# Layer 0 of a four-layer network: a unit's sums are folded half a group sooner, their copies and some small transfers change queues

## The chip, the cores and the metric

One core of a Trainium2 chip runs the whole network in one launch. The metric is the device time of that core in microseconds (us), the median of three runs. Five engines work side by side, each taking its own instructions in order: TensorE (PE, matrix products), VectorE (DVE), ScalarE (ACT), GpSimd (POOL) and SyncE (SP). ACT, POOL and SP also issue the DMAs; which one issues a DMA decides in whose order it stands.

## The reference

Four layers run one after the other on images of 512 channels. Only layer 0 is touched by the change. It is attention with a sampled set of 64 keys for each of 2 x 8 heads and a learned position bias, and the bias is what costs time:

```python
pos = grid_q[:, :, None, :] - grid_kv[:, None, :, :]          # 1024 queries x 64 keys x 2
bias = jnp.sign(pos) * jnp.log1p(jnp.abs(pos))
bias = jax.nn.relu(bias @ cpb_w1 + cpb_b1)                    # 2 -> 128
bias = jax.nn.relu(bias @ cpb_w2 + cpb_b2)                    # 128 -> 128
bias = (bias @ cpb_w3 + cpb_b3)                               # 128 -> 1
sim = jnp.einsum('bhid,bhjd->bhij', qh, kh) + bias
attn = jax.nn.softmax(sim, axis=-1)
out = jnp.einsum('bhij,bhjd->bhid', attn, vh)
```

So a small network with 128 hidden values runs on 16 heads x 1024 queries x 64 keys. The keys' places come from a convolution of the queries (`off`), and `grid_sample` fetches the keys' inputs there.

## The kernel before

**Units, groups, half groups.** Layer 0 is a hand-ordered program (`layer0`): PE, DVE, ACT and POOL take their instructions in the order in which the Python code writes them. A unit `u` (0 to 15) is one head of one image. It has eight groups `o` (0 to 7) of eight keys, and each group has two halves of four keys. The loop at L190 runs over these half groups; there are 16 in a unit, and I number them `it` 0 to 15, so `it = 2 * o + half`. Units 2p and 2p+1 share a "pair" (one tile of 128 channels), whose queries, key places, keys and values are made ahead by generators in the list `front`; the softmax and output of a finished unit are generators in the list `after`. At the end of each half group one step of `after` is run, and one of `front` as well if that step of `after` allows it.

**One half group.** `first_hidden` (L739 to L762) makes the first hidden layer on DVE for the next half group. `second_hidden` (L764 to L818) then multiplies with `w2s` on PE (L780) in four quarters `q`, each into a PSUM tile `hp` of which there are three; ACT reads each with a Relu (L794) and so frees the PSUM tile. Quarter 0 is followed by a second ACT pass (L797 or L799). The quarters are added up: 1 += 0 by an accumulating DMA that POOL issues (L804), 3 += 2 by POOL (L808), and 3 += 1 by POOL one half group later (`join`, L811). In some halves DVE takes a quarter instead of ACT: `late`, quarter 3 (L789; second halves of groups 1 and 2, in odd units of groups 1 to 4), and `early`, quarter 2 (L792; second halves of groups 0 and 7).

**Folds and sums.** Both halves' quarter 3 are the two parts of one tile with the tag `two`, of which there are three, so group `g` writes into the tile of group `g-3`. A group's tile is folded over its partitions 128 to 64 to 32 to 16 by three accumulating DMAs that POOL issues (L814, L836, L839), and then SP copies the 16 rows that are left into a sum tile (L846, two DMAs). These later steps are generators in `refolds`: `refold_more` runs a step at quarter 1 of each later half group, and the copies at the end of the half group named in the entry, here the second half of group `g+2`. Each unit has two sum tiles, `sum{u}_0` for even and `sum{u}_1` for odd groups, with the tag `sum` and three buffers. The tiles go round these three buffers in the order 0_0, 0_1, 1_0, 1_1 and so on, so `sum{u}_1` lies where `sum{u-1}_0` was.

**A finished unit's sums.** While unit `u` runs, the two sum tiles of unit `v = u - 1` become the bias of its attention (for `u` from 1 to 14): ACT multiplies by a sign (L222), POOL issues two accumulating folds (`keys_rows`, L851 and L853, 128 to 64 to 32 partitions), and ACT issues two DMAs that copy the 32 rows into `rows` (L857). Before the change this is written at the end of `it` 3 for `sum_0` and `it` 5 for `sum_1`, the folds come at `it` 5 and 6, and 7 and 8, the copies at the end of `it` 7 and 9, and `attend` starts at the end of `it` 11.

**Small transfers.** For each pair `offsets` writes the logarithms (`logs`) and the sampling places (`spots`) to DRAM, and `sampled` reads `spots` back into all partitions (`at`); DVE uses `at` at L604. `load` brings `lb` back from `logs` (ACT issues three of four, L676). The first three of these go through `send`, which issues on SP:

```python
def send(self, to, what):
    with self.behind(self.gathered):
        self.nc.sync.dma_start(to, what)
```

Of the kernel before, what the change touches and what calls it, by code (L numbers as in the profile page):

```python
# [18 lines left out]
P = 128  # L19
# [4 lines left out]
HF = 512  # L24
# [33 lines left out]
class Net:  # L58
# [40 lines left out]
    def layer0(self):  # L99


        nc, io = self.nc, self.io
        with ExitStack() as ctx:
# [45 lines left out]
            with self.tc.manual_schedule(engines=engines):  # L149
# [40 lines left out]
                for i, (u, o, half) in enumerate(quads):  # L190
                    self.half = half
                    if o == 2 and half == 1 and u % 2 == 0 and u // 2 + 1 < BP:
                        nxt = pairs[u // 2 + 1]
                        front += [self.offsets(nxt, u // 2 + 1, ps), self.sampled(nxt, u // 2 + 1, ps)]
                    h1 = ready
                    if i + 1 < len(quads):
                        if quads[i + 1][1:] == (7, 0) and u + 1 < 2 * BP:
                            self.advance(front, lambda: "logs" in pairs[(u + 1) // 2])
                        ready = self.first_hidden(*quads[i + 1], pairs, tables)
                    last_set = u == last and o >= 4  # L200
                    if half == 0:
                        if o == 0:
                            before, sums = sums, []
                        if o % 4 == 0:
                            group = []
                        if i + 2 < len(quads):
                            both = self.two_tiles(f"h2_{u}_{o}3")
                            group.append([both[:, 0, :], both[:, 1, :], both])
                        else:
                            group.append([self.four_rows(f"h2_{u}_{o}{n}3") for n in range(2)])  # L210
                        if o < 2:
                            sums.append(self.four_rows(f"sum{u}_{o}"))
                    self.second_hidden(i, u, o, half, h1, group[-1], i + 1 == len(quads), last_set)
                    if half == 1 and not last_set:
                        end = i + (3 if u == last else 4)
                        self.refolds.append((i + 2, end, end, self.refold(group[-1][2], sums[o % 2], o // 2, u == last)))
                    v = u - 1
                    if half == 1 and o in (1, 2) and 0 <= v < last - 1:
                        z = before[o - 1]
                        if o == 1:  # L220
                            rows = self.soft.tile([P, HF], F32, tag="pt", name=f"rows{v}")
                        nc.scalar.activation(z, z, AF.Copy, scale=self.last_sign)  # L222
                        self.refolds.append((i + 2, i + 4, i + 4, self.keys_rows(z, rows, o - 1)))
                    if half == 1 and o == 2 and v >= 0:
                        sims[v] = ps_s.tile([P, HF], F32, tag="sim", name=f"sim{v}")
                        if v == last - 1:
                            self.sum_product(sims[v], self.thrice, True, before)
                        self.advance(front, lambda: "v" in pairs[v // 2])
                        self.keys_queries(v, pairs[v // 2], sims[v], v < last - 1)
                    if v >= 0 and (o, half) == ((5, 1) if v < last - 1 else (2, 1)):  # L230
                        if v == 8:
                            self.advance(after, lambda: False)
                            att = [apool.tile([P, N], F32, tag=f"att{t}", name=f"att{v}_{t}") for t in range(CT)]
                        after.append(self.attend(v, pairs[v // 2], sims[v], att, ps, rows if v < last - 1 else None))
                        if v % 8 == 7:
                            after.append(self.projection(ps, att, ow, v // 8))
                    elif half == 1 and u == last and o == 5:
                        sims[u] = ps_s.tile([P, HF], F32, tag="sim", name=f"sim{u}")
                        self.sum_product(sims[u], self.twice[:, 16:48], True, sums)
                    elif half == 1 and u == last and o == 7:  # L240
                        self.sum_product(sims[u], self.folded[:, 8:40], False, [one[0] for one in group[:2]])
                    self.refold_more(i, True)
                    if not self.step(after):
                        self.step(front)
# [156 lines left out]
    def offsets(self, m, bt, ps):  # L401
# [3 lines left out]
        nc = self.nc  # L405
# [33 lines left out]
        o = self.bank[:, 256:258]  # L439
        for par in range(2):  # L440
            rows = slice(par * DH, (par + 1) * DH)
            nc.tensor.matmul(o[rows, :], lhsT=ge[rows, :], rhs=self.colr("pw", 2)[rows, :], start=True, stop=True)
        tanh, at = self.bank[:, 258:260], self.bank[:, 260:262]
# [15 lines left out]
        log = self.fpool.tile([P, 2, W], F32, tag="log", name=f"log{b}{t}")  # L459
# [14 lines left out]
        else:  # L474
            nc.vector.tensor_tensor(log, log, sign, ALU.mult)
        logs = self.dram.tile([P, 2 * W], F32, tag="logs", name=f"logs{b}{t}")
        self.send(logs, log.rearrange("p d x -> p (d x)"))
        spots = self.dram.tile([P, 2], F32, tag="spots", name=f"spots{b}{t}")

        g = self.fpool.tile([P, 2], F32, tag="g", name=f"g{b}{t}")  # L480
        nc.scalar.activation(g, at, AF.Identity, scale=W / 2.0, bias=self.grid[:, G_MID : G_MID + 1])
        self.send(spots, g)
        m["log"], m["logs"], m["spots"] = log, logs, spots
        yield

# [1 line left out]

        return nullcontext() if ins is None else self.tc.issue_after(ins.ins)

    def send(self, to, what):  # L490

        with self.behind(self.gathered):
            self.nc.sync.dma_start(to, what)

# [92 lines left out]
    def sampled(self, m, bt, ps):  # L587
# [3 lines left out]
        nc = self.nc  # L591
        b, t = divmod(bt, CT)
        spots = self.fone.tile([P, 2 * NJ, 2], F32, tag="spots", name=f"at{b}{t}")
        self.send(spots, m["spots"].rearrange("k d -> (k d)").partition_broadcast(P))
        if "xT" not in m:
            self.sampling(m, bt)
            nc.scalar.copy(m["xT"], self.turn(m, bt, ps))
# [25 lines left out]
        for n in range(NB):  # L623
            for par in range(2):
                rows = slice(par * DH, (par + 1) * DH)
# [17 lines left out]
        for par in range(2):  # L643
            rows = slice(par * DH, (par + 1) * DH)
# [25 lines left out]
    def load(self, u, c, pairs, early):  # L670

        logs = pairs[u // 2]["logs"].rearrange("(a j c i) e -> a c j (i e)", a=2, j=2, c=4)[u % 2, c]
        got = self.lpool.tile([P, 2, 8, 2, W], F32, tag="logs", name=f"lb{u}{c}")
        to, what = got.rearrange("p j i d x -> p j (i d x)"), logs.unsqueeze(0).to_broadcast([P, 2, 16 * W])
        if early:
            self.nc.scalar.dma_start(to, what)  # L676
        else:
            self.send(to, what)
        return got

    def table(self, u, o, pairs, tables):
# [166 lines left out]
    def keys_rows(self, z, to, jj):  # L848

        nc = self.nc  # L850
        nc.gpsimd.dma_start(z[0::2], z[1::2], accum_op=ALU.add)  # L851
        yield
        nc.gpsimd.dma_start(z[0::4], z[2::4], accum_op=ALU.add)  # L853
        yield
        for h in range(2):
            at = h * NJ + jj * 32
            nc.scalar.dma_start(to[at : at + 32, :], z[0::4, h * HF : (h + 1) * HF])  # L857

    def sum_product(self, sim, lhsT, start, zs):

# [1348 lines left out]
```

## Time and profile before

| what | value |
|---|---|
| time, median of 3 runs | 3255.38 us (3253.26 to 3260.8) |
| time of the profiled execution | 3257.2 us |
| its span from first to last instruction | 3255.5 us |
| half groups of layer 0 | from about 27 us to about 1935 us |
| granted TensorE clock, mean | 0.996 |
| PE busy over the span | 98% |
| ACT, DVE, POOL busy over the span | 59%, 76%, 73% |

Layer 0 fills the first 24 of the page's 40 slices. The other layers are untouched by the change, so the difference of the two kernels is to be looked for in the first 1935 us. A busy share is a mean over a stage; what delays an engine is read from its idle time and from what ended it.

### The profile page before, as it was taken

What the parts mean: (1) busy time and instruction counts of PE and PEld (TensorE: products, weight loads), DVE (VectorE), ACT (ScalarE), POOL (GpSimd) and SP (SyncE); (2) the same over time, 40 slices, a digit from 0 to 9 for tenths busy, and PEclk for the clock granted to TensorE, in tenths of its full rate; (3) what the DMA queues carried; (4) which work ended last, traced back from release to release, by engine and by line L of the source; (5) the groups of instructions that cost most, each with busy time, mean ns of one, the idle gap of its engine ahead of it and who ended that gap; (6) DMA issues with size and microseconds to landing.
All of it is one profiled execution on the core that took longest, in us unless ns stands there. A gap on an engine that the chain in (4) does not pass through costs nothing.

```text
span 3255.5 us, 58764 instructions
## 1 busy us (share of the span) xinstructions
PE 3205.5 (98%) x23956; PEld 1216.4 (37%) x23956; DVE 2475.8 (76%) x2834; ACT 1906.6 (59%) x1985; POOL 2361.8 (73%) x1664
## 2 busy tenths in 40 slices
PE   9999999999999999999999999999999999999999
PEld 4323233233333333343332334444455533455333
DVE  7878878878878678888887865575565689855897
ACT  7877777877877577787877761111231466213662
POOL 7989988989989789989988965333243458634575
PEclk9999999999999999999999999999999999999999
DMA  6787787787787677787787863111000100000001
GB/s 168 161 174 156 155 172 156 155 165 162 160 166 158 130 155 158 154 169 164 156 168 157 164 142 116 47 44 39 1 1 1 40 1 1 15 1 14 1 1 53
DMA packets 96590, 341.91 MB, mean 105 GB/s; under 512 B 19888, under 2 KB 22064, under 8 KB 79216
## 3 DMA queue, kind: packets, MB, share of 16 engines
q0 software_dynamic: 56224, 244.88, 39.5%
q1 hardware_dynamic: 23600, 62.68, 5.8%
q10 hardware_dynamic: 16480, 30.42, 3.4%
q8 instruction: 193, 3.16, 0.4%
q14 instruction: 93, 0.76, 0.1%
HBM read 67.37 MB, written 4.46 MB: 22 GB/s over the span
## 4 chain that ended last, share of the span: by engine, by line
PE 62%; POOL 17%; DMA 7%; DVE 7%; issue 4%; ACT 2%; ACTq 0%; SPq 0%; POOLq 0%; DVEq 0%
PE hp L780 25%; POOL h L811 7%; PE s L1742 5%; PE o L1771 5%; POOL h L808 5%; DMA h<-h 3%; POOL h L804 2%; DMA sum<-h 2%; ACT h L794 2%; PE qk30P L1517 1%; PE qk20P L1517 1%; PE m_7P L1026 1%; PE m_5P L1026 1%; PE m_4P L1026 1%; PE m_2P L1026 1%
## 5 line engine op out<-in xcount | busy, mean ns | idle before, releaser
L780 PE MATMUL hp<-h,w2s 128*32 128x512 f32 x16384 | 1803.3, 595 | 35.1 <-ACT h L794 32.8
L794 ACT ACTIVATE h<-hp,magb 128x1024 f32<-128x1024 f32 x950 | 1044.5, 1109 | 428.8 <-PE hp L780 327.3
L753 DVE CUSTOM_DVE_ANT_1 h<-tx,bank 128x1024 f32<-128x1024 f32 (+1 forms) x1028 | 1180.7, 1211 | 120.3 <-PE hp L780 84.4
L780 PEld LDWEIGHTS hp<-h,w2s 128*32 128x32 f32 x16384 | 564.1, 110 | 1240.3 <-issue 1074.6
L811 POOL TENSOR_TENSOR h<-h,h 128x1024 f32<-128x1024 f32 x254 | 739.2, 2910 | 15.9 <-DMA h<-h 13.8
L808 POOL TENSOR_TENSOR h<-h,h 128x1024 f32<-128x1024 f32 x209 | 656.8, 3142 | 6.1 <-ACT h L794 6.1
L804 POOL DMA_DIRECT2D h<-h x227 | 295.3, 1301 | 139.5 <-ACT h L794 138.2
L1746 ACT ACTIVATE e<-s 128x1024 f32<-128x1024 f32 x256 | 262.0, 1025 | 180.9 <-PE s L1742 175.3
L1771 PE MATMUL o<-e,v 64*64 64x512 f32 x2048 | 265.2, 589 | 2.2 <-DVE q L1810 2.2
L1742 PE MATMUL s<-q,k 64*64 64x512 f32 x2048 | 265.9, 591 | 0.0
L799 ACT ACTIVATE h<-h,flip 128x1024 f32<-128x1024 f32 x182 | 209.6, 1152 | 6.0
L1753 POOL TENSOR_TENSOR some<-some,e 128x1024 f32<-128x1024 f32 x64 | 167.6, 2618 | 26.7 <-ACT e L1746 24.2
L836 POOL DMA_DIRECT2D h<-h x124 | 174.3, 1405 | 16.6 <-DMA h<-h 9.6
L1751 POOL TENSOR_TENSOR some<-e,e 128x1024 f32<-128x1024 f32 x32 | 76.1, 2378 | 141.3 <-DVE sum L1760 106.3
L814 POOL DMA_DIRECT2D h<-h x127 | 162.9, 1283 | 6.0 <-issue 3.9
L1758 DVE TENSOR_TENSOR sum<-sum,e 128x1024 f32<-128x1024 f32 x64 | 123.7, 1932 | 29.8 <-ACT e L1746 27.1
L839 POOL DMA_DIRECT2D h<-h x120 | 137.3, 1144 | 5.9 <-DMA h<-h 5.4
L996 POOL TENSOR_TENSOR mlp_w<-mlp_w 128x512 f32<-128x512 f32 x16 | 22.6, 1413 | 159.4 <-DMA mlp_w<-in_mlp_w 127.3
L1771 PEld LDWEIGHTS o<-e,v 64*64 64x64 f32 x2048 | 77.8, 133 | 145.0 <-issue 135.2
L1742 PEld LDWEIGHTS s<-q,k 64*64 64x64 f32 x2048 | 76.5, 133 | 133.2 <-issue 117.6
L789 DVE SCALAR_TENSOR_TENSOR h<-hp,under,h 128x1024 f32<-128x1024 f32 x46 | 59.0, 1283 | 86.2 <-ACT h L794 75.9
L1092 ACT ACTIVATE mh<-mh,cols 128x512 f32<-128x512 f32 x64 | 46.1, 721 | 124.3 <-DVE mh L1110 64.3
(595 smaller groups left out, 3621.0 us busy)
## 6 DMA issues: line engine op xcount, KB each, us to landing
h<-h POOLq DMA_DIRECT2D x354, 512.0 KB, 5.8
h<-h POOLq DMA_DIRECT2D x124, 256.0 KB, 4.5
lb<-logs ACTq DMA_DIRECT2D x47, 512.0 KB, 6.0
mlp_w<-in_mlp_w SPq DMA_DIRECT2D x16, 1024.0 KB, 4.8
h<-h POOLq DMA_DIRECT2D x120, 128.0 KB, 3.6
sum<-h SPq DMA_DIRECT2D x240, 64.0 KB, 3.5
lb<-logs SPq DMA_DIRECT2D x16, 512.0 KB, 7.2
sum<-sum POOLq DMA_DIRECT2D x28, 256.0 KB, 6.7
```

Of the source, the lines that this page charges most:

```text
L753: self.nc.vector._custom_dve(TENSOR_ADD_SAT, out=h1[r][:, k, cut, :], in0=x[:, 4 * half + 2 * r + k, :].unsqueeze(1).to_broadcast([P, H // ...
L780: nc.tensor.matmul(hp[rows, cut], lhsT=self.l0w2[:, 32 * q : 32 * q + 32], rhs=h1[k][:, cut], start=True, stop=True)
L794: nc.scalar.activation(y, hp, AF.Relu, bias=self.magb[:, q, 0:1])
L799: nc.scalar.activation(y, y, AF.Copy, scale=self.flip)
L804: self.added = pool.dma_start(y, ys[0], accum_op=ALU.add)
L808: self.added = (vec if final else pool).tensor_tensor(y, y, ys[2], ALU.add)
L811: (vec if final else pool).tensor_tensor(z, z, other, ALU.add)
L836: nc.gpsimd.dma_start(both[0::4], both[2::4], accum_op=ALU.add)
L1742: nc.tensor.matmul(s[halves[c], par, :], lhsT=ks[p][rows, at : at + DH], rhs=qs[p][rows, cut], start=True, stop=True)
L1746: nc.scalar.activation(e, s, AF.Exp, scale=DH**-0.5)
L1753: nc.gpsimd.tensor_tensor(state["some"], state["some"], e, ALU.add)
L1771: nc.tensor.matmul(o[halves[par], r, :], lhsT=v[n // 2][rows, n % 2, at : at + DH], rhs=e[rows, par, :], start=(n == 0), stop=(n == NB - 1),)
```

## The change

The signs and folds of a finished unit's sums are written half a group sooner: at the end of `it` 2 and `it` 4 rather than 3 and 5. The first fold follows one half group later (`it` 3 and 5, before 5 and 7), the second two half groups behind the first (`it` 5 and 7, before 6 and 8), the copies to `rows` at the end of `it` 6 and 8 (before 7 and 9), now issued by SP instead of ACT. `attend` starts at the end of `it` 10 instead of 11. For all pairs but the first, `spots`, `logs` and `at` are issued by ACT instead of SP, and one `front` step apart from each other: `logs` one step after `spots`, `at` one step later, and DVE's use of `at` again a step after.

In the order of the instructions this moves, of each of 14 units: on ACT the sign from behind the second half's quarters to behind the first half's quarter 3, and the four copies away; on SP the four copies in, two ahead of the `sum_1` copies of group 1 and two ahead of the `sum_0` copies of group 2; on POOL the four folds forward; and the output product of the attention on PE from after `it` 0 of the next unit to after `it` 15. DVE's use of `at` moves later, in units 3, 5 and 7 from the end of `it` 8 to that of `it` 11, and the rest of `sampled` behind it. No instruction's size changes; the counts are the same but for the queue.

```diff
--- before.py
+++ after.py
@@ -215,19 +215,19 @@
                         end = i + (3 if u == last else 4)
                         self.refolds.append((i + 2, end, end, self.refold(group[-1][2], sums[o % 2], o // 2, u == last)))
                     v = u - 1
-                    if half == 1 and o in (1, 2) and 0 <= v < last - 1:
+                    if half == 0 and o in (1, 2) and 0 <= v < last - 1:
                         z = before[o - 1]
                         if o == 1:
                             rows = self.soft.tile([P, HF], F32, tag="pt", name=f"rows{v}")
                         nc.scalar.activation(z, z, AF.Copy, scale=self.last_sign)
-                        self.refolds.append((i + 2, i + 4, i + 4, self.keys_rows(z, rows, o - 1)))
+                        self.refolds.append((i + 1, i + 4, i + 4, self.keys_rows(z, rows, o - 1)))
                     if half == 1 and o == 2 and v >= 0:
                         sims[v] = ps_s.tile([P, HF], F32, tag="sim", name=f"sim{v}")
                         if v == last - 1:
                             self.sum_product(sims[v], self.thrice, True, before)
                         self.advance(front, lambda: "v" in pairs[v // 2])
                         self.keys_queries(v, pairs[v // 2], sims[v], v < last - 1)
-                    if v >= 0 and (o, half) == ((5, 1) if v < last - 1 else (2, 1)):
+                    if v >= 0 and (o, half) == ((5, 0) if v < last - 1 else (2, 1)):
                         if v == 8:
                             self.advance(after, lambda: False)
                             att = [apool.tile([P, N], F32, tag=f"att{t}", name=f"att{v}_{t}") for t in range(CT)]
@@ -474,12 +474,14 @@
         else:
             nc.vector.tensor_tensor(log, log, sign, ALU.mult)
         logs = self.dram.tile([P, 2 * W], F32, tag="logs", name=f"logs{b}{t}")
-        self.send(logs, log.rearrange("p d x -> p (d x)"))
         spots = self.dram.tile([P, 2], F32, tag="spots", name=f"spots{b}{t}")
 
         g = self.fpool.tile([P, 2], F32, tag="g", name=f"g{b}{t}")
         nc.scalar.activation(g, at, AF.Identity, scale=W / 2.0, bias=self.grid[:, G_MID : G_MID + 1])
-        self.send(spots, g)
+        self.send(bt == 0, spots, g)
+        if bt > 0:
+            yield
+        self.send(bt == 0, logs, log.rearrange("p d x -> p (d x)"))
         m["log"], m["logs"], m["spots"] = log, logs, spots
         yield
 
@@ -487,8 +489,11 @@
 
         return nullcontext() if ins is None else self.tc.issue_after(ins.ins)
 
-    def send(self, to, what):
-
+    def send(self, sync, to, what):
+
+        if not sync:
+            self.nc.scalar.dma_start(to, what)
+            return
         with self.behind(self.gathered):
             self.nc.sync.dma_start(to, what)
 
@@ -591,7 +596,9 @@
         nc = self.nc
         b, t = divmod(bt, CT)
         spots = self.fone.tile([P, 2 * NJ, 2], F32, tag="spots", name=f"at{b}{t}")
-        self.send(spots, m["spots"].rearrange("k d -> (k d)").partition_broadcast(P))
+        if bt > 0:
+            yield
+        self.send(bt == 0, spots, m["spots"].rearrange("k d -> (k d)").partition_broadcast(P))
         if "xT" not in m:
             self.sampling(m, bt)
             nc.scalar.copy(m["xT"], self.turn(m, bt, ps))
@@ -675,7 +682,7 @@
         if early:
             self.nc.scalar.dma_start(to, what)
         else:
-            self.send(to, what)
+            self.send(True, to, what)
         return got
 
     def table(self, u, o, pairs, tables):
@@ -850,11 +857,12 @@
         nc = self.nc
         nc.gpsimd.dma_start(z[0::2], z[1::2], accum_op=ALU.add)
         yield
+        yield
         nc.gpsimd.dma_start(z[0::4], z[2::4], accum_op=ALU.add)
         yield
         for h in range(2):
             at = h * NJ + jj * 32
-            nc.scalar.dma_start(to[at : at + 32, :], z[0::4, h * HF : (h + 1) * HF])
+            nc.sync.dma_start(to[at : at + 32, :], z[0::4, h * HF : (h + 1) * HF])
 
     def sum_product(self, sim, lhsT, start, zs):
 
```

## The prediction

> **What bounds the kernel now.** I read the page first, then the list of waits, then the timeline of one place at which the waits pile up.
>
> ```profile
> PE 3205.5 (98%) x23956; PEld 1216.4 (37%) x23956; DVE 2475.8 (76%) x2834; ACT 1906.6 (59%) x1985; POOL 2361.8 (73%) x1664
> L780 PE MATMUL hp<-h,w2s 128*32 128x512 f32 x16384 | 1803.3, 595 | 35.1 <-ACT h L794 32.8
> ```
>
> PE is busy for 98%, and layer 0's product (L780) is more than half of all its time. The last column matters: PE sat idle for 35.1 us before these products, 32.8 of them until ACT had freed a PSUM tile. Those microseconds are all that a change of waits in layer 0 can bring directly. The list of waits, over the span, for PE, ACT and DVE, then SP's own list, says who made ACT late:
>
> ```profile
> ACT h L794 <- DMA sum<-h: 61.7, 18, 6.0
> DVE sampling L604 <- DMA at<-spots: 39.2, 5, 9.9
> PE hp L780 <- ACT h L794: 32.8, 18, 6.4
> ```
>
> ```profile
> SPq L846 <- DMA rows<-sum: 111.4, 23, 22.8
> ```
>
> ACT waits 18 times for a sum copy (us in total, times, longest), which must have read the group tile that ACT writes next. SP, which issues that copy, waits 23 times for `rows<-sum`: the copy's target lies where the sum tile was that `rows` is read from. The timeline of unit 3 shows the chain, ACT first, then SP, then PE (start, duration, what; in brackets the idle time before it):
>
> ```profile
> 429.05 2.25 ACT L794 ACTIVATE h<-hp,magb 128x1024 f32<-128x1024 f32 x2
> 433.99 1.92 ACTq L857 DMA_DIRECT2D rows<-sum  x2
> 435.95 0.60 ACTq L676 DMA_DIRECT2D lb<-logs  x1
> 436.66 1.12 ACT L794 ACTIVATE h<-hp,magb 128x1024 f32<-128x1024 f32 x1 [5.36 <-issue]
> 437.81 1.15 ACT L799 ACTIVATE h<-h,flip 128x1024 f32<-128x1024 f32 x1
> 438.86 2.10 ACT L794 ACTIVATE h<-hp,magb 128x1024 f32<-128x1024 f32 x2
> 445.44 2.12 ACT L794 ACTIVATE h<-hp,magb 128x1024 f32<-128x1024 f32 x2 [4.48 <-DMA sum<-h]
> ```
>
> ```profile
> 439.40 1.35 SPq L846 DMA_DIRECT2D sum<-h  x2
> 440.84 0.64 SPq L493 DMA_DIRECT2D at<-spots  x1
> ```
>
> ```profile
> 437.83 1.92 PE L780 MATMUL hp<-h,w2s 128*32 128x512 f32 x16 [0.81 <-ACT h L794]
> 440.01 3.64 PE L780 MATMUL hp<-h,w2s 128*32 128x512 f32 x32 [0.26 <-ACT h L794]
> 446.61 3.93 PE L780 MATMUL hp<-h,w2s 128*32 128x512 f32 x20 [2.96 <-ACT h L794]
> ```
>
> ACT stands from 431.3 on, because the `rows` DMA in its order waits for the second fold (landed 434.0). The two DMAs land at 439.2; 0.2 us later SP issues the copy of group 1, though that group's last fold had landed at 433.8. The copy lands at 445.3, and only then ACT may write quarter 3 of `it` 8. PE lost 0.81 and 2.96 us. The same stands in every unit from 1 to 14: `it` 8, quarter 3, ACT gap 3.1 to 8.4 us. PE's gaps there, read off its timeline, are in units 1, 3, 5, 7, 13: 3.36, 0.81 + 2.96, 6.40, 2.36, 1.84 (17.7 us); in units 2, 4, 6, 8, 10, 12, 14: 1.55, 2.25, 1.25, 1.18, 1.79, 1.66, 2.60 (12.3 us); none in 9 and 11. Sum 30.0 of the 32.8.
>
> After the four longest gaps PE runs slow. The windows right behind them (length, busy times, granted clock, DMA):
>
> ```profile
> 209.40:215.20 5.80, 5.77 (x28) 1.39 (x32) 0.00 (x0) 4.33 (x4) 5.36 (x4) 0.51 0.58 126
> 446.60:450.60 4.00, 3.99 (x24) 1.14 (x28) 2.75 (x3) 3.97 (x4) 4.00 (x4) 0.58 0.98 198
> 688.60:693.00 4.40, 4.35 (x24) 1.05 (x28) 4.24 (x6) 3.89 (x4) 3.95 (x4) 0.50 0.33 75
> 1773.80:1778.40 4.60, 4.58 (x28) 1.29 (x32) 0.00 (x0) 4.13 (x4) 4.60 (x6) 0.63 0.95 176
> ```
>
> The clock fell to 0.51, 0.58, 0.50 and 0.63, so 5.80 x 0.49 + 4.00 x 0.42 + 4.40 x 0.50 + 4.60 x 0.37 = 8.4 us more were lost inside "busy" time: 6.7 in units 1, 3, 5 and 1.7 in unit 14. In all the stall costs 38.4 us: 24.4 in odd units, 14.0 in even ones.
>
> **What the Trainium skill says.** "TensorE: Matmul & The Clock Gate", What's actually happening: an idle window of about 3.4 us puts PE at half its clock, and it needs about as long to come back; the window runs freely. The trace agrees: gaps of 2.60 to 6.40 us were followed by half clock, 2.36 us was not. "Perfetto Trace Analysis", Optimization Strategy: a gap that repeats on the engine that should be full can mean too few buffers. So it is here: three sum tiles. "DMA: Bandwidth & Descriptors", Issuing engines are not separate DMA queues: another issuing engine saves only issue time. The trace says more for this kernel: an engine whose next DMA waits stands still with all behind it (ACT's 5.36 us).
>
> **The change part by part.**
>
> *Copies to `rows` half a group sooner, on SP.* Taking unit 10: fold 2 of `sum_0` is issued at 1284.0 now, and lands at 1287.9. Written one `it` earlier, at the place of the present fold 1 (1276.8), it lands 3.8 us (the median of fold 2) later, near 1281. SP issues two DMAs (0.52 us each, median of L857) and they land 3.4 us later, near 1286. The last fold of group 1 landed at 1287.5, so the copy is now released by its own fold, issues near 1287.6 instead of 1294.1 and lands 3.5 to 5.9 us later (the median, and what it took here): 1291 to 1293.5. ACT would be ready for quarter 3 near 1295. The wait is gone with 1.5 to 4 us to spare, and PE has two more PSUM tiles of 1.73 us each (6.93 us a half group over four quarters) before it feels ACT. What stood in ACT's order behind `rows` (`lb`, quarter 0) is free too. Gain up to 38.4 us.
>
> *What stands behind the copies on SP.* The copies of groups 1 and 2 now queue behind `rows`. `sum_1`'s fold 2 at `it` 7 lands near 1296, its `rows` issue then, and group 2's copy was not released before 1303.4. Cost nothing; if fold 2 came 6 us later, group 1's copy would slip with it.
>
> *Signs.* 28 of 1.14 us (L222) move from a half in which DVE takes quarter 3 to one in which ACT takes all four. The sign stands behind quarter 3: quarter 0 starts 1.1 + 1.14 - 1.73 = 0.5 us late, quarter 1 about 1.0 (the second pass adds 1.15), under the 2.4 us that the three PSUM tiles give. It adds no wait: quarter 3 already waits for the same sum copy. Nothing, or 1 us each where quarter 3 was late anyway (units 3 and 12, 2.5 and 3.4 us at `it` 4): 0 to 3 us lost.
>
> *Folds on POOL.* The same 56 issues. POOL's waits for the first fold (L853, 9.2 us in 11 times) go, since the second comes two half groups later; four issues move to where POOL waits for ACT (about 3 us in `it` 4 of most units). DMA: 256 KB more at `it` 3, next to a 512 KB `lb` load, and as much less at `it` 7. Between nothing and a microsecond a unit either way on POOL; I take nothing.
>
> *`spots`, `logs`, `at` on ACT.* 21 issues of about 0.5 us into the 1.3 us that ACT has free in most halves; each finds its data landed, one or more half groups (6.9 us) after the write. DVE's wait for `at` (39.2 us in five odd units, at the same `it` 8 as the stall) goes, as `at` has two half groups instead of one. Without that the odd units could not gain their share.
>
> *`attend` half a group sooner.* Its exponential (with a table load in odd units) moves from ACT's `it` 13 to 12, the output product from `it` 0 to 15, where ACT has a quarter less to read. The tile `rows` shares a buffer with the turned weights that this product reads, so it comes free sooner as well. All of it is hidden by the 1.3 us that ACT has free in each of these halves; without that cover the table load and the exponential would cost about 2 us in 7 units. Nothing.
>
> *The next thing that is late.* From `it` 9 to 15 POOL is never idle in even units, and the copy of group 5 then lands only 0.1 to 0.9 us before ACT needs it at `it` 0 of the next unit. PE, earlier by 1.2 to 2.6 us, meets this. POOL too is earlier, by the L853 wait and one issue, so part remains: from none to all of the 14.0 us; I take 60%, 8.4 us. In odd units POOL waits for ACT for 2 to 5 us at `it` 10, so it follows, and I take all 24.4.
>
> Sum: 3257.2 - 24.4 - 8.4 = 3224.4 for the profiled execution, which stands 1.8 us above the median; against the median 3222.6.
>
> **The rivals.**
>
> 1. *All of it* (0.25): even units keep their 14.0 and small gaps go too: 3255.4 - 38.4 = 3217; at most 6 us below that (PE's other idle time before L780).
> 2. *Half* (0.15): POOL's backlog, or the slower folds with the added DMA at `it` 3, turns the stall into one at quarter 3 of the next `it` 0. Only the odd units' part comes, less half: about 12 to 20 us, 3239. For it: the 0.1 us slack. Against it: ACT never waits for POOL's own sums in this trace.
> 3. *Slower* (0.05): SP becomes the place of the stall. It issues in order, and `rows` ahead of group 1's copy waits for fold 2. If POOL reaches that fold over 6 us later than reckoned, the copy issues no sooner than now, behind two SP issues more (1.1 us), and ACT pays 1.1 us in 14 units, with the clock falling in more of them (about 2 us each): 15 to 30 us, 3275. Against it: POOL has idle time in `it` 4 and 6.
> 4. *Nothing* (0.05): both effects cancel, 3255.
>
> **How the numbers follow.** The first forecast, 3222, has 0.50. Within 0.2%, 6.5 us, a measurement of this kernel can't tell a difference. Faster by more: 0.50 + 0.25 + 0.15 = 0.90; same 0.05; slower 0.05. The range reaches from 3209 (rival 1's end, rounded) to 3240 (rival 2), the rest is left out.
>
> **What would show it.** SP's waits for `rows<-sum` gone or short; ACT's wait at quarter 3 of `it` 8 near the 0.6 us of an undisturbed half; PE's idle time before L780 from 35 to below 12 us, no window at half clock after 200 us; DVE's wait for `at` gone; and what is left of the idle time at `it` 0 of odd units. The prediction is wrong if SP's copies of group 1 still issue after `rows` and late, or if PE's idle time goes and the span does not.

## The result, and the profile after

| | before | after |
|---|---|---|
| median of 4 runs | 3257.34 us (3253.26 to 3260.80) | 3215.34 us (3214.34 to 3220.19) |
| span of the profiled execution | 3255.5 us | 3212.9 us |

The ratio is 0.9874, 95% interval 0.9857 to 0.9892: the changed kernel is 1.3% faster. The forecast was 3222. The time is 7 us below it, inside the range, and nearer to the first rival (3217). Two runs, one of `e6` and one of `e8` below, had a granted clock of 0.65 and 0.56 and took 4803 and 5643 us; they are left out of all medians and ratios.

The two lines of the page that answer to the first ones shown of before (PE busy over the span; the product of layer 0, with PE's idle time ahead of it in the last column):

```profile
PE 3193.2 (99%) x23956; PEld 1212.1 (38%) x23956; DVE 2473.5 (77%) x2834; ACT 1904.7 (59%) x1985; POOL 2364.1 (74%) x1664
L787 PE MATMUL hp<-h,w2s 128*32 128x512 f32 x16384 | 1790.7, 593 | 4.9 <-ACT h L801 3.6
```

Idle time ahead of the product fell from 35.1 to 4.9 us, by 30.2, and busy time on the same 16384 products from 1803.3 to 1790.7, by 12.6. Together that is 42.8 of a span that is 42.6 shorter: nothing is left for the other layers. The list of waits of after over the span, ACT and PE (us in total, times, longest):

```profile
ACT h L801 <- DMA sum<-h: 10.9, 5, 4.2
...
PE hp L787 <- ACT h L801: 3.6, 4, 1.4
```

ACT's waits for a sum copy went from 61.7 us in 18 to 10.9 in 5. A wait of DVE for `at<-spots` (39.2 us before) is not in the list any more, nor is POOL's for the first fold (9.2 us). SP's own list:

```profile
SPq L865 <- DMA sum<-sum: 181.4, 28, 8.7
...
SPq L853 <- DMA rows<-sum: 27.7, 13, 4.2
```

SP now does the waiting for the second fold, 28 times, two for each of 14 units, and what is left of its waits for `rows` (27.7 of 111.4 us) is no longer the last one: in unit 3 it waits 4.2 us for `rows` and then 1.4 us more for the fold of the group that it copies. The timeline of unit 3 in after, the same three engines as in the prediction, ACT, SP and PE (start, duration, what, idle time before it):

```profile
425.59 1.11 ACT L801 ACTIVATE h<-hp,magb 128x1024 f32<-128x1024 f32 x1 [2.31 <-DMA logs<-log]
426.73 1.15 ACT L806 ACTIVATE h<-h,flip 128x1024 f32<-128x1024 f32 x1
427.79 2.34 ACT L801 ACTIVATE h<-hp,magb 128x1024 f32<-128x1024 f32 x2
431.42 2.15 ACT L801 ACTIVATE h<-hp,magb 128x1024 f32<-128x1024 f32 x2 [1.28 <-DMA h<-h]
```

```profile
416.55 1.33 SPq L865 DMA_DIRECT2D rows<-sum  x2
423.64 1.31 SPq L853 DMA_DIRECT2D sum<-h  x2
```

```profile
416.75 30.68 PE L787 MATMUL hp<-h,w2s 128*32 128x512 f32 x284
```

The two `rows` copies issue 7 us ahead of group 1's sum copy and land at 422.1; that group's last fold lands at 423.6, and the copy issues at once. In all 14 units it issues within 0.2 us of its own fold's landing. ACT's gap at quarter 3 of `it` 8 is 1.28 us instead of 4.48. Both halves of the copy had landed only at 431.3, so in units 1, 3, 5 and 7 it is still the last to arrive, but late by less than PE's PSUM tiles cover: PE runs 30.68 us through without a gap. Over all units the gap is 0.07 to 1.86 us. No product of layer 0 runs at half clock in after. In before 88 of them did, for 18.6 us in four stretches, of which half, 9.3 us, is lost.

One new wait is in the trace, of POOL:

```profile
POOL tx L698 <- DMA lb<-logs: 4.8, 1, 4.8
```

It is pair 5's `logs`, in unit 9: they are now written one step after `spots`, at 1174.76 on ACT, and the `lb` that SP fetches from them lands only at 1185.14. Three of PE's four gaps are in unit 10 (0.70, 0.18 and 1.45 us).

### The profile page after: what moved, and what is told of

Its sections match the earlier page's. It is cut to its first block, busy times and chain, and to the rows that moved or that the text cites. A ratio compares the mean times of both kernels' runs of the same rounds, so it can differ in the third digit from the quotient of the medians.

```text
span 3212.9 us, 58771 instructions
## 1 busy us (share of the span) xinstructions
PE 3193.2 (99%) x23956; PEld 1212.1 (38%) x23956; DVE 2473.5 (77%) x2834; ACT 1904.7 (59%) x1985; POOL 2364.1 (74%) x1664
## 4 chain that ended last, share of the span: by engine, by line
PE 78%; DVE 8%; POOL 6%; DMA 3%; issue 2%; ACT 1%; SPq 0%; DVEq 0%; POOLq 0%; ACTq 0%
PE hp L787 41%; PE s L1750 5%; PE o L1779 5%; POOL h L818 2%; DVE h L760 2%; POOL h L815 2%; DMA h<-h 2%; PE qk20P L1525 2%; PE qk30P L1525 2%; PE m_2P L1034 1%; PE m_7P L1034 1%; PE m_6P L1034 1%; PE m_4P L1034 1%; PE m_1P L1034 1%; PE qk31P L1525 1%
## 5 line engine op out<-in xcount | busy, mean ns | idle before, releaser
L787 PE MATMUL hp<-h,w2s 128*32 128x512 f32 x16384 | 1790.7, 593 | 4.9 <-ACT h L801 3.6
L1766 DVE TENSOR_TENSOR sum<-sum,e 128x1024 f32<-128x1024 f32 x64 | 124.9, 1952 | 28.5 <-ACT e L1754 25.7
L1100 ACT ACTIVATE mh<-mh,cols 128x512 f32<-128x512 f32 x64 | 46.1, 721 | 124.3 <-DVE mh L1118 64.3
```

Of the source, the lines that this page charges most:

```text
L787: nc.tensor.matmul(hp[rows, cut], lhsT=self.l0w2[:, 32 * q : 32 * q + 32], rhs=h1[k][:, cut], start=True, stop=True)
```

## The experiments

The change has three parts: the **times** (signs, folds and `attend` half a group sooner, the second fold two half groups behind the first), the **rows** copies on SP, and the **small** transfers on ACT. Three theories of where the time sat: **A**, the sum copy of group 1 has to wait for the `rows` copies, because a sum tile can't be overwritten before it is read; **B**, ACT stands still behind its own `rows` DMAs; **C**, the small transfers keep SP and DVE late. The first seven kernels are each part alone and each pair of parts, and the sign alone.

Medians here stand beside runs of the kernel before on the same chip (3253.67 us for `e1`, `e2`, `e3`, `e5`; 3255.22 for `e4`, `e6`, `e7`, `e8`; 3253.74 for `e9`, `e11`, `e12`), and all their ratios are to those; after stands beside the 3257.34 us above.

| run | times | rows | small | median, us | ratio, 95% interval |
|---|---|---|---|---|---|
| e1_timing | x | | | 3227.74 | 0.9916, 0.9902 to 0.9930 |
| e2_rows_sp | | x | | 3263.35 | 1.0027, 1.0019 to 1.0035 |
| e3_small | | | x | 3253.39 | 0.9994, 0.9981 to 1.0007 |
| e4_timing_small | x | | x | 3229.33 | 0.9923, 0.9911 to 0.9935 |
| e5_timing_rows | x | x | | 3220.72 | 0.9895, 0.9878 to 0.9912 |
| e6_rows_small | | x | x | 3265.83 | 1.0027, 1.0017 to 1.0037 |
| after | x | x | x | 3215.34 | 0.9874, 0.9857 to 0.9892 |

**Times alone.**

```diff
-                    if half == 1 and o in (1, 2) and 0 <= v < last - 1:
+                    if half == 0 and o in (1, 2) and 0 <= v < last - 1:
...
-                        self.refolds.append((i + 2, i + 4, i + 4, self.keys_rows(z, rows, o - 1)))
+                        self.refolds.append((i + 1, i + 4, i + 4, self.keys_rows(z, rows, o - 1)))
...
-                    if v >= 0 and (o, half) == ((5, 1) if v < last - 1 else (2, 1)):
+                    if v >= 0 and (o, half) == ((5, 0) if v < last - 1 else (2, 1)):
...
         nc.gpsimd.dma_start(z[0::2], z[1::2], accum_op=ALU.add)
         yield
+        yield
```

> The kernel before with the change's times alone: signs, folds and copies half a group sooner, second fold two half groups behind, attend half a group sooner; the copies stay on ACT, the small transfers on SP. Theory A (the stall is the sum copy of group 1 waiting until rows<-sum_0 has read the buffer it goes into): fold 2 lands near it 6, ACT issues the copies at the end of it 6, they land before group 1's last fold; SP's waits for rows<-sum fall from 111 us to under 20, PE's idle time before L780 from 35 to under 12 us; 3215 to 3225 us. Theory B (ACT standing behind the rows DMAs in its own order is what counts): ACT still issues them, at most half the gain, 3235 to 3250 us. Theory C (logs, spots and at on SP delay the sum copies and DVE): odd units keep their stall, PE idle 17 us or more, 3235 to 3245 us.

Measured: 0.84% faster, 26 of the 42 us, 3 us above A's range and under those of B and C. The visible stall is gone, as the page's line of this kernel shows:

```profile
L780 PE MATMUL hp<-h,w2s 128*32 128x512 f32 x16384 | 1800.9, 593 | 5.2 <-ACT h L794 2.5
```

Its idle time is that of after (5.2 against 4.9), no product runs at half clock, and yet PE is busy for 10.2 us more on the same products. Those are waits that the page can't show. Each product is recorded as 593 ns long, but in an unbroken stretch four of them start 7 ns apart, and the next four 429 ns after the first. The last of the four so ends 183 ns after the next four have begun, and a delay that fits into this overlap counts as busy. Taken from the starts, idle time left out, the delays between one four and the next sum to 22.6 us in `e1` and 12.2 us in after (only where no other product of PE stands between them). From here on I therefore also compare when the first product of each half group starts; the lists of waits alone would have called this kernel as good as after.

**Rows alone.**

```diff
-            nc.scalar.dma_start(to[at : at + 32, :], z[0::4, h * HF : (h + 1) * HF])
+            nc.sync.dma_start(to[at : at + 32, :], z[0::4, h * HF : (h + 1) * HF])
```

> The kernel before with nothing changed but the queue of the rows copies: SP instead of ACT, folds at their old times. Theory A: fold 2 lands as late as before, the copies leave SP at once and land about 2 us sooner than before, group 1's sum copy still waits for them; ACT's gap at it 8 shrinks from 3 to 8 us to about 2 to 5 us, part of which three PSUM tiles absorb; 3230 to 3245 us. Theory B: ACT no longer stands, all of the gain, 3214 to 3222 us. Theory C: no change or slower, 3250 to 3262 us.

Measured: 0.27% slower, where A had a gain. The timelines of unit 5 show how, in that unit. Before, ACT and then SP:

```profile
672.65 1.44 ACTq L857 DMA_DIRECT2D rows<-sum  x2
674.13 0.59 ACTq L676 DMA_DIRECT2D lb<-logs  x1
```

```profile
678.08 2.45 SPq L846 DMA_DIRECT2D sum<-h  x2
```

With `rows` on SP, ACT and then SP:

```profile
670.23 0.37 ACTq L676 DMA_DIRECT2D lb<-logs  x1
```

```profile
673.40 1.84 SPq L857 DMA_DIRECT2D rows<-sum  x2
681.70 1.42 SPq L846 DMA_DIRECT2D sum<-h  x2
```

ACT no longer stands behind `rows`, as B has it. So in this unit it issues the 512 KB load of `lb` 3.2 us ahead of `rows` instead of 1.5 us behind, and the two `rows` copies land 7.0 and 7.6 us after their issue instead of 4.4 and 4.8. The sum copy waits for them and goes out 3.6 us later. ACT's gap at quarter 3 grew from 8.35 to 10.01 us.

The units differ, though. In units 2, 4, 6 and 10 `lb` still leaves at least 2.4 us behind `rows`, the sum copy goes out sooner after its own fold, and ACT's gap falls from 3.5 to 4.5 us to at most 1.7, as A had it. In the odd units but 9, and in 14, the gap grew. That the load ahead is what slows the copies is a reading of unit 5 and was not tested by a run of its own; it isn't the whole account, as in unit 3 `lb` had landed before `rows` was issued, and the copies still took 5.3 and 5.0 us. What the run shows is that freeing ACT alone, at the old times, is no gain: the sum copy waits for when the read has landed, not for who issues it.

**Small transfers alone.**

```diff
-        self.send(logs, log.rearrange("p d x -> p (d x)"))
-        self.send(spots, g)
+        self.send(bt == 0, spots, g)
+        if bt > 0:
+            yield
+        self.send(bt == 0, logs, log.rearrange("p d x -> p (d x)"))
...
+        if not sync:
+            self.nc.scalar.dma_start(to, what)
+            return
...
-        self.send(spots, m["spots"].rearrange("k d -> (k d)").partition_broadcast(P))
+        if bt > 0:
+            yield
+        self.send(bt == 0, spots, m["spots"].rearrange("k d -> (k d)").partition_broadcast(P))
```

> The kernel before with nothing changed but spots, logs and at on ACT, each a front step apart. Theory A: group 1's sum copy waits for rows as before, so the stall at it 8 stays in all 14 units; DVE's wait for at (39 us) goes, which is worth little while ACT stalls at the same place; 3248 to 3258 us. Theory B: the same or slower, ACT issues more. Theory C: odd units lose their stall, PE idle from 35 to about 17 us and little half clock, 3228 to 3240 us.

Measured: no change (3253.39 against 3253.67). C alone is no account of the gain.

**Two parts at a time.** Each is the changed kernel with one of the three diffs above taken back: `rows` on ACT again, small transfers on SP again, or the old times.

> The whole change with the rows copies left on ACT: times and small transfers. Theory A: the copies leave ACT at the end of it 6 and land before group 1's last fold, no wait for rows; 3214 to 3222 us, PE idle before its product under 8 us. Theory B: ACT still issues four copies a unit, 3230 us or more.

> The whole change without its small transfers: times and the rows copies on SP, while logs, spots and at stay on SP. Theory A: the wait for rows is gone as in the whole change; at stands on SP behind one sum copy less late, DVE's wait for at shrinks to a few us in odd units; 3214 to 3224 us. Theory B: 3214 to 3222 us. Theory C: the odd units keep their stall, 3235 to 3245 us.

> The whole change without its times: rows copies on SP, small transfers on ACT, signs and folds where they were. Theory A: fold 2 lands late, group 1's sum copy still waits for rows, ACT's gap at it 8 is 2 to 5 us in most units, partly absorbed: 3228 to 3242 us, SP still waits after the rows copies. Theory B with C: 3214 to 3222 us.

Measured: of A's three ranges only that for `e5` came true. `e4` is 7 us above A's and just under the 3230 us of B; `e6` is 24 us above A's. Without the times the kernel is slower than before (`e6`), although both queue changes are in it; six stretches at half clock stand in its trace, and PE's idle time ahead of the product is 44.3 us. With the times, `rows` on SP is worth 14 us (from `e4` to after, intervals apart) and 7 us where the small transfers stay on SP (from `e1` to `e5`, same chip, intervals overlapping at the edge). The small transfers are worth 5 us on top (from `e5` to after), whose intervals overlap, and nothing while `rows` is on ACT (from `e1` to `e4`, 1.6 us slower, intervals overlap too). In `e4`, ACT's waits for a sum copy are 25.1 us in 12, against 10.9 in 5 in after, and the products have 10.2 us more of busy time:

```profile
ACT h L801 <- DMA sum<-h: 25.1, 12, 4.4
```

```profile
L787 PE MATMUL hp<-h,w2s 128*32 128x512 f32 x16384 | 1800.9, 593 | 6.8 <-ACT h L801 4.7
```

So B may have a share once the times are in, since in `e4` ACT issues the `rows` copies in its own order. Whether its standing there or the later sum copies cost the 14 us, the runs don't tell apart.

By half groups the profiled executions say more. This is how much longer than in after the units take, counted from product start to product start, odd and even units apart, and how much of it lies in `it` 9, where PE feels the stall at the end of `it` 8:

| | before | e2 rows | e3 small | e6 rows, small | e1 times | e4 times, small | e5 times, rows |
|---|---|---|---|---|---|---|---|
| odd units 1 to 13, us | 37.8 | 46.1 | 12.8 | 38.4 | 14.2 | 12.2 | 12.8 |
| of it in `it` 9 | 29.8 | 39.3 | 13.3 | 37.2 | 4.7 | 5.7 | 4.6 |
| even units 2 to 14, us | 5.8 | -1.2 | 20.4 | 15.8 | -3.6 | 0.3 | -6.6 |
| of it in `it` 9 | 15.7 | 8.1 | 20.3 | 20.3 | 0.5 | 0.5 | -1.1 |

Each column is one execution, and in the first four, where the stall is still in, runs of one kernel differ by 8 to 20 us. In those four `attend` has its old place; for that alone the even units show about 5 us less (9.9 less at `it` 15, 4.6 to 4.8 more at `it` 0).

In odd units, the ones with sampling, the last 12 to 14 us go only when all three parts are in; in `e3` what remains is the stall itself, smaller than before in odd units and larger in even ones. In `e5` DVE still waits for `at`:

```profile
DVE sampling L604 <- DMA at<-spots: 21.7, 5, 7.0
```

In unit 5, 5.1 of the 5.2 us that it takes more than in after lie in `it` 9 and 10, behind such a wait of 7.0 us. The small transfers move three DMAs and also DVE's use of `at`; which of these counts was not taken apart.

In even units the times do it all, and the small transfers cost a few microseconds: 4.4 of the 6.6 between `e5` and after are in unit 10, where POOL's wait for pair 5's `lb` is.

**The sign alone.**

```diff
+                    if half == 0 and o in (1, 2) and 0 <= v < last - 1:
+                        nc.scalar.activation(before[o - 1], before[o - 1], AF.Copy, scale=self.last_sign)
...
-                        nc.scalar.activation(z, z, AF.Copy, scale=self.last_sign)
```

> The kernel before with the two signs of a unit moved half a group sooner on ACT and all else where it was. This prices the sign behind quarter 3 in a half in which ACT takes all four quarters. Reckoned: nothing to 3 us slower, 3255 to 3260 us. If the sign were felt each time (28 times about 1.1 us): 3270 to 3290 us.

Measured: 3257.56 us, 2.3 above the 3255.22 of before, ratio 1.0012 (1.0003 to 1.0021, or 1 to 7 us). The sign brings nothing by itself and costs next to nothing.

**The distance between the two folds.** In the changed kernel, three half groups instead of two, then one:

```diff
-                        self.refolds.append((i + 1, i + 4, i + 4, self.keys_rows(z, rows, o - 1)))
+                        self.refolds.append((i + 1, i + 5, i + 5, self.keys_rows(z, rows, o - 1)))
...
         yield
         yield
+        yield
```

> The whole change with the second fold three half groups behind the first instead of two: first fold, signs, queues and attend as in the whole change; only the landing of fold 2, and with it of rows, is again about as late as before. Theory A: the stall at it 8 comes back in part, ACT's gap there 2 to 5 us, SP's sum copies of group 1 leave right after the rows landing; 3225 to 3240 us. Theories B and C: nothing of theirs is touched, 3213 to 3218 us.

Measured: 3244.8 us, 0.9966 (0.9954 to 0.9978), 28.5 us slower in the profiled execution than after. The stall is back at its old place with everything else of the change left in. Unit 3 of this kernel, ACT and then SP:

```profile
442.38 2.12 ACT L801 ACTIVATE h<-hp,magb 128x1024 f32<-128x1024 f32 x2 [7.60 <-DMA sum<-h]
```

```profile
428.24 2.39 SPq L866 DMA_DIRECT2D rows<-sum  x2
436.61 1.91 SPq L853 DMA_DIRECT2D sum<-h  x2
```

`rows` goes out when the second fold has landed (428.1), lands at 436.5, and the sum copy issues 0.1 us later, 5.4 us after its group's last fold (431.2). Of the 28.5 us, 23 are lost at this place in units 1, 3, 5 and 7; in even units ACT's gap is at most 3.0 us, and PE hardly feels it (1.0 us in `it` 9). Since `rows` is issued by SP here and the small transfers are on ACT, B and C have no part in this stall. It is the clearest run for A, and it cost 5 us more than the upper end that I had given.

```diff
-                        self.refolds.append((i + 1, i + 4, i + 4, self.keys_rows(z, rows, o - 1)))
+                        self.refolds.append((i + 1, i + 3, i + 3, self.keys_rows(z, rows, o - 1)))
...
         yield
-        yield
```

> The whole change with the second fold one half group behind the first instead of two, and the copies to rows a half group sooner. If all that counts is that rows has landed before group 1's last fold has: nothing to gain, 3213 to 3218 us, though POOL waits for the first fold again (about 9 us in all, as before the change). If the distance of the folds is itself worth something on POOL: 3218 to 3226 us.

Measured: 3217.34 us, 0.9889 (0.9874 to 0.9905), span 3212.8. In unit 3 `rows` now issues at 410.4 instead of 416.6, and the sum copy still goes out when its own fold has landed (421.9). Sooner than soon enough brings nothing.

**`attend` back at its old place, and pair 5's `logs` without the step.** From the half-group times I had read that `attend` half a group sooner costs about 5 us at `it` 15. `e11` is the changed kernel with the first edit, `e12` with both:

```diff
-                    if v >= 0 and (o, half) == ((5, 0) if v < last - 1 else (2, 1)):
+                    if v >= 0 and (o, half) == ((5, 1) if v < last - 1 else (2, 1)):
...
-        if bt > 0:
+        if bt not in (0, 5):
             yield
         self.send(bt == 0, logs, log.rearrange("p d x -> p (d x)"))
```

> The whole change with attend written at the end of it 11 as before the change, not it 10, so that the attention's output product stands on PE after it 0 of the next unit rather than after it 15. Counted by the starts of PE's products, the half groups it 15 of units 1 to 14 take 14.5 us more after the change, and it 0 about 9 us less once the move of the projection in unit 9 is taken out. If that place is what costs: 5 us less than the whole change, 3208 to 3212 us. If it is only counting: 3213 to 3217 us.

> As the one with attend at it 11, and for the pair of units 10 and 11 logs leaves ACT in the same step as spots. In the changed kernel POOL waits 4.8 us for lb at the end of unit 9, because logs was written one step later, and PE loses 0.70 and 1.45 us in unit 10. Expected: these gaps gone, 2 us less than with attend at it 11 alone; 3206 to 3211 us.

Measured: `e11` 3219.02 us, 0.9891 (0.9877 to 0.9905): no gain, so that reading fell. The output product had moved from one half group's count to another's; the time for which it holds up layer 0's products is 17.3 us in after, 16.1 in `e11` and 13.2 in before, so most of the increase is not due to the place. `e12` 3212.22 us, 0.9870 (0.9854 to 0.9885), all four runs from 3210.92 to 3213.68. POOL's wait for `lb` and PE's gaps in unit 10 aren't in its trace, and the page's line reads:

```profile
L787 PE MATMUL hp<-h,w2s 128*32 128x512 f32 x16384 | 1787.6, 593 | 4.7 <-ACT h L801 3.5
```

This is 7 us under `e11`, from which only the `logs` edit sets it apart, though the two intervals just overlap; against after (3 us) they overlap by far. It has the lowest time of the study, and I can't claim that it beats after.

A fourth sum tile, which would take A's wait away with the old times, was not tried. So the wait was shown by making it longer (`e8`), not by taking the shared tile away.

## Why the prediction was right, and where its sum was off

**The place and the mechanism: right.** The prediction put the cost at quarter 3 of `it` 8, through ACT's wait for the sum copy of group 1 and that copy's wait for `rows<-sum_0`. In after the copy follows its own fold within 0.2 us in every unit, and `e8` brings the stall back by making `rows` late again. "Perfetto Trace Analysis", Optimization Strategy, which the prediction used for a gap that repeats, led to the right buffer; the cure here was an earlier reader and not another buffer.

**When things land: right in unit 10, too short in some others.** Counted from the landing of group 1's last fold in unit 10, the working had fold 2 landing 6.5 us before it, `rows` 1.5 before, the copy issued 0.1 after and landed 3.5 to 6 after, and ACT ready for quarter 3 at 7.5. In after that fold lands at 1256.8; fold 2 landed 7.9 us before, `rows` 4.6 and 2.2 before, the copy landed 3.9 and 5.6 after, and quarter 3 starts at 8.5 behind a gap of 0.56 us. In units 1, 3, 5 and 7 the second half of the copy lands 7.0 to 7.9 us after the fold, above the upper figure, and ACT waits 1.3 to 1.9 us, which the PSUM tiles take up.

**The stall's cost: 38.4 us said, 42.8 measured.** The gaps were right: 30.0 said, 30.2 gone in all. The half clock was 9.3 us, where 8.4 had been read from windows that cut the slow stretches short. The other 3.3 are the sum of two things that the prediction did not have as terms. Delays too short for the page to show, counted as for `e1` and with the half clock taken out, fell by 7.5 us (19.7 to 12.2). Against that, PE's other products hold up those of layer 0 for 4.2 us more, nearly all of it at the output product of the attention.

**Odd and even units: the term that was mis-sized.** The forecast took 24.4 us from odd units and 8.4 from even ones (60% of 14.0, the rest handed on). Measured by product starts over whole units they gave 37.8 and 5.8. The odd term was 13 us too small. In `it` 9 alone odd units gave 29.8, so 5 us are the stall itself. The rest lies elsewhere in these units, 6.9 of it in `it` 10, as in `e5`. The term was made of the stall's gaps and clock alone, while DVE's wait for `at` was put down as "without that the odd units could not gain their share", a cover and no cost of its own. The pairs say that it has one: with the times in, 12 to 14 us stay in odd units until the small transfers and `rows` have both left their old queues, mostly in waits that end inside "busy" time.

The even total is near the forecast for another reason than it gave. In `it` 9 even units gave 15.7 us, all of the 14.0 and more. Little of it went where the prediction looked, to the sum copy of group 5: in after this copy lands at least 0.3 us ahead of quarter 3 at the next unit's `it` 0, but for units 10 and 15, in which ACT waits 2.89 and 0.83 us there. About 5 us went at the unit's ends, where the output product stands (9.9 more at `it` 15, 4.6 less at `it` 0), and some in unit 10, behind the late `lb`. That 3222 came within 7 us is so in part luck: the odd term was too small and the even one a little too large.

**Edits costed at nothing.** Signs: right (`e7`: 2.3 us, in the 0 to 3 said, though its interval reaches to 7). Folds on POOL: right, and its wait of 9.2 us went. `attend`: right (`e11`). `rows` on SP was counted with the times, as one step. Apart, it is worth 7 to 14 us with the times and is a loss without them. `spots`, `logs` and `at` on ACT were called hidden because each finds its data landed. On ACT that held but for two waits for `logs` (4.6 us, under PE's cover), but `logs` a step later made one `lb` late, and nothing in the prediction looked at who reads `logs` next.

**The rivals.** "Slower" needed SP to become the place of the stall through a second fold 6 us later than reckoned. `e8` brings that case about, by a whole half group: it costs 28.5 us against after and takes most of the gain, but doesn't end above before. "Half" needed POOL's backlog; at `it` 0 ACT waits only in units 10 and 15. "All of it" was the best of the four: at the stall's place even units did keep their 14.0. What it did not have are the odd units' larger gain, and the loss at the even units' ends.

**The clock.** The prediction read its trace as in agreement with the window of about 3.4 us that it quotes: 2.60 us and more were followed by half clock, 2.36 was not. Gaps of 2.60 and 2.96 us are shorter than that window, and over all runs there is no such line. A gap of 2.02 us (`e3`, at 680.6) was followed by half clock, and gaps of 2.92 (`e7`, at 1768.3) and 3.69 us (`e8`, at 209.5) were not. So a gap of 2 to 4 us may cost the clock or not, and where one falls has a part of luck.

## What to carry to other kernels

When an engine waits for a buffer, follow the wait to the last reader of what the buffer holds, and move that reader ahead of the moment at which the rest is ready: how far ahead didn't matter here (`e9`), and 3 to 8 us behind cost two thirds of the gain (`e8`). Before a waiting DMA is taken out of an engine's order, list what stands behind it and when that will then start, because a stopped queue may be holding a large load back from a small urgent copy (`e2`, unit 5). Try the parts of such a change in pairs and not only alone: two of the three parts here did nothing or harm by themselves, and are worth 12 us together once the third is in (from `e1` to after).

## What the runs showed of the hardware that was not expected

- PE's busy time hides short waits. With equal idle time (5.2 and 4.9 us) and no half clock in either, the same 16384 products took 1800.9 us of busy time in `e1` and 1790.7 in after. Product starts show the difference (22.6 against 12.2 us of delays), busy shares don't.
- "DMA: Bandwidth & Descriptors", Issuing engines are not separate DMA queues, lets another issuing engine save only issue time. Here the same two copies, moved from ACT to SP, landed 7.0 and 7.6 us after issue instead of 4.4 and 4.8 in unit 5, where the move let a 512 KB load go first, and 2.2 to 3.0 us after issue in units 2, 4, 6 and 10, where it didn't. In this kernel the move so changed more than the issue time.
- The slow stretches in the clock's record that follow idle gaps in layer 0 last 3.41 or 6.83 us in every run that has them, after gaps from 2.02 us (`e3`) to 7.18 us (`e2`).
